# An S4 macaron block on one core: the opening by chunks, packing in lumps, and the S4 response as two products

## The chip, the core and the metric

The kernel runs on one NeuronCore of a Trainium2 chip. The core has a matrix engine (PE, TensorE), a vector engine (DVE), an activation engine (ACT), GpSimd (POOL) and SyncE (SP), which here issues most transfers. [...] The metric is the device time of one execution in microseconds (us), taken as the median of several; the profile shows one further execution.

## The reference

The input is 2048 tokens of 1024 features. Three blocks follow each other, each on a layer norm of `x`:

```python
x = x + 0.5 * ffn(layernorm(x))          # 4-bit weights, 1024 -> 2752 -> 1024
x = x + s4(layernorm(x))                 # long convolution along the features
x = x + 0.5 * ffn(layernorm(x))          # the same weights again

# ffn: W[k, n] = scale[k // 128, n] * (w4[k, n] - (z4[k // 128, n] + 1))
h = silu(xf @ Wg) * (xf @ Wu);  out = h @ Wd

# s4: the response K (1024 taps) from 64 poles, then a causal convolution plus D * u
at_roots = c * (k00 - k01 * (1 / (1 + k11)) * k10);  K = ifft(at_roots).real
y = irfft(rfft(u, 2048) * rfft(K, 2048), 2048)[..., :1024] + D * u
```

## The kernel before

The tokens are cut into four blocks of 512. Each of the two feed-forward layers on each block is a "job", eight in all (`JOBS`). A job has an up stage of 64 steps and a down stage of 44. The 2752 gate and up columns are cut into eight waves (`WAVES`): five of six units (a unit is 128 columns of gate or up), two of four and one of five. A wave has eight steps, one for each group of 128 rows that share a scale. In a step, each unit gets two matmuls of 128 x 512 into its own PSUM bank: one with the high part of the turned rows (`xTh`), one with the low part (`xTl`). Then the bank is multiplied in place by the ratio of two groups' scales (`scaled`, L618 to L622), on ACT for gate units and on DVE for up units, and only then can the next step's matmul add to it.

The weights arrive as 4-bit words. In job 0 they are unpacked once: for wave w, `fetch` (L441) loads the words and `fetch_zeros` (L448) the zero points, broadcast from a table in DRAM; `split` (L472, through `signed_bytes`, L455) makes bytes of them in six DVE operations; `dequantize` (L495) copies each of eight nibble positions into a contiguous tile `q` (a pool of four buffers) and stores it to DRAM as rows of `wq`. Every step of every job then loads 128 rows of bytes (`load_bytes`, L572) and casts them to fp32 (`make_weights`, L589): on POOL, in job 0 for steps 1, 2 and 5 of a wave on ACT, and the first one on DVE. A load of wave w waits for all eight stores of that wave. When a wave ends, `gated` (L675) makes the hidden rows and splits them into high and low halves, `hh` and `hl`, on POOL.

The order of work is made of three things. The function `at` hangs pieces of side work on steps of the up and down stages. A scheduler then orders the instructions of each engine by when it thinks them ready. `in_order_of_writing` (L140) ties the instructions of the named engines, so that they stay in the order in which they were written. `first_weights` (L537) hangs the packing of waves 1 to 7 on the steps of job 0: for wave w, with `s0 = 8 * w - 12`, it fetches at `s0 - 5`, splits in six pieces over `s0 - 3` to `s0 - 1`, and casts one nibble position a step from `s0` on.

Before all steps stands `start` (L1434): it loads the zero words, the rows of block 0 and the words of waves 0 and 1, makes the zero-point tables and sends them through DRAM, takes the moments of the four row tiles on DVE (`moments`, L175), packs wave 0, normalizes the first half of each row tile on ACT in two passes (`less_mean`, `by_deviation`), and turns it tile by tile on PE (`turn`, L230). The second halves follow in steps 0 to 3 (`second_half`, L1428). The pieces of wave 0 that step 0 needs go straight into a tile (`first_tile`), by transfers that POOL issues.

In job 1, `s4_tables` (L1014) makes the S4 tables in 63 pieces of side work. One part is `s4_response` (L940): it forms the 1024 taps of K from a table `se` of 128 x 2 x 8 numbers and two cosine and sine tables of 128 x 1024, one row of 128 taps at a time; two matmuls (cosine, sine) for each of eight rows, with one column of `se` as weights. The taps lie in a single partition and are stored to DRAM as one row, which `s4_toeplitz` reads back in 128 shifted copies.

## Time and profile before

| what | value |
|---|---|
| time, median of 3 (lowest to highest) | 2151.65 us (2150.85 to 2152.0) |
| the profiled execution: its own time, and its span | 2152.6 us, 2150.7 us |
| busy: PE, DVE, ACT, POOL | 2092.5, 1704.3, 1422.3, 1062.5 us |
| moved by DMA | 132.49 MB |
| chain of work that ended last | PE 87%, DVE 7%, POOL 2% |
| PE busy in 29 to 64, 64 to 88, 88 to 110.5, 110.5 to 133.3 us | 29.91, 22.66, 21.86, 22.45 us |
| DVE busy in the same stretches | 26.50, 22.41, 18.95, 19.70 us |

A table by stage gives, for each stretch of the span, the busy time of PE, of PE's weight loads, of DVE, ACT and POOL, the granted clock of PE, the share of the DMA engines and GB/s. The chain of work that ended last is followed back from the last instruction to whatever released each one; its lines are start, length and what. A timeline line is start, length, engine, source line, operation, tiles, shapes and count, with the idle time before it in brackets. A line of a group of instructions ends in busy time, mean duration in ns, and the engine's idle time before it with what ended most of that. SPq is an issue of a transfer by SP. Matmuls overlap, so the duration of one is longer than the distance to the next.

### The profile page before, as it was taken

What the parts mean: (1) busy time and instruction counts of PE and PEld (TensorE: products, weight loads), DVE (VectorE), ACT (ScalarE), POOL (GpSimd) and SP (SyncE); (2) the same over time, 40 slices, a digit from 0 to 9 for tenths busy, and PEclk for the clock granted to TensorE, in tenths of its full rate; (3) what the DMA queues carried; (4) which work ended last, traced back from release to release, by engine and by line L of the source; (5) the groups of instructions that cost most, each with busy time, mean ns of one, the idle gap of its engine ahead of it and who ended that gap; (6) DMA issues with size and microseconds to landing.
All of it is one profiled execution on the core that took longest, in us unless ns stands there. A gap on an engine that the chain in (4) does not pass through costs nothing.

```text
span 2150.7 us, 30258 instructions
## 1 busy us (share of the span) xinstructions
PE 2092.5 (97%) x9748; PEld 1425.5 (66%) x9748; DVE 1704.3 (79%) x2783; ACT 1422.3 (66%) x2233; POOL 1062.5 (49%) x1420
## 2 busy tenths in 40 slices
PE   4999999999999999999999999999999999999998
PEld 2555675577867568665776568676686766866576
DVE  7888978578788877778777788878788787777776
ACT  5887677646654776676767767646776467767765
POOL 3767747554344543455335553454534455345642
PEclk9999999999999999999999999999999999999999
DMA  4425232112111211212221121112111121121111
GB/s 136 116 85 148 78 92 59 32 54 76 41 41 54 89 53 39 78 33 58 87 80 36 31 74 37 38 52 77 35 36 41 52 93 48 44 81 36 34 35 57
DMA packets 163544, 132.49 MB, mean 62 GB/s; under 512 B 22252, under 2 KB 151029, under 8 KB 163376
## 3 DMA queue, kind: packets, MB, share of 16 engines
q1 hardware_dynamic: 162528, 129.12, 19.9%
q8 instruction: 79, 1.29, 0.3%
q10 hardware_dynamic: 592, 1.25, 0.2%
q14 instruction: 89, 0.73, 0.1%
q0 software_dynamic: 256, 0.10, 0.0%
HBM read 104.79 MB, written 25.50 MB: 61 GB/s over the span
## 4 chain that ended last, share of the span: by engine, by line
PE 87%; DVE 7%; POOL 2%; issue 1%; DMA 1%; ACT 1%; SPq 0%; DVEq 0%; ACTq 0%; POOLq 0%
PE pg L650 53%; PE po L713 27%; PE pc L1040 3%; DVE pg L622 2%; PE pb L735 1%; PE pb L1040 1%; PE pt L224 1%; DVE po L622 1%; PE st L224 1%; POOL w_down L598 0%; DVE hf L680 0%; POOL qd L531 0%; PE s_k L954 0%; DVE even L465 0%; ACT g L677 0%
## 5 line engine op out<-in xcount | busy, mean ns | idle before, releaser
L620 ACT ACTIVATE pg<-pg,rat 128x512 f32<-128x512 f32 x1240 | 787.3, 661 | 435.7 <-PE pg L650 434.8
L622 DVE TENSOR_TENSOR pg<-pg,rat 128x512 f32<-128x512 f32 x1168 | 776.1, 693 | 182.4 <-PE pg L650 178.4
L650 PE MATMUL pg<-xTh,w_up 128*128 128x512 f32 x2752 | 852.3, 438 | 6.3 <-DVE pg L622 4.5
L650 PE MATMUL pg<-xTl,w_up 128*128 128x512 f16 x2752 | 723.2, 383 | 13.6 <-DVE w_up L594 6.6
L650 PEld LDWEIGHTS pg<-xTh,w_up 128*128 128x128 f32 x2752 | 520.2, 189 | 185.2 <-DVE pg L622 18.3
L598 POOL CAST w_up<-b 128x768 fp32r<-128x768 int8 (+2 forms) x487 | 377.6, 781 | 529.6 <-PE pg L650 428.6
L713 PE MATMUL po<-hl,w_down 128*128 128x512 f32 x1344 | 538.8, 403 | 9.4 <-DVE po L622 7.3
L620 ACT ACTIVATE po<-po,ratd 128x512 f32<-128x512 f32 x660 | 431.0, 662 | 158.9 <-PE po L713 158.7
L713 PE MATMUL po<-hh,w_down 128*128 128x512 f32 x1344 | 522.4, 391 | 0.0
L622 DVE TENSOR_TENSOR po<-po,ratd 128x512 f32<-128x512 f32 x620 | 427.0, 697 | 96.6 <-PE po L713 92.6
L650 PEld LDWEIGHTS <-w_up 128*128 128x128 bf16 x2752 | 228.4, 99 | 335.3 <-issue 153.1
L598 POOL CAST w_down<-bd 128x512 fp32r<-128x512 int8 x352 | 222.5, 634 | 405.3 <-PE po L713 340.7
L713 PEld LDWEIGHTS po<-hl,w_down 128*128 128x128 f32 x1344 | 251.9, 188 | 86.2 <-DVE po L622 20.5
L713 PEld LDWEIGHTS po<-hh,w_down 128*128 128x128 f32 x1344 | 252.8, 188 | 45.2
L684 POOL TENSOR_TENSOR hl<-hf,hh 128x512 fp32r<-128x512 f32 x168 | 217.0, 1292 | 7.9
L680 DVE SCALAR_TENSOR_TENSOR hf<-pg,rat,g 128x512 f32<-128x512 f32 x168 | 122.9, 748 | 47.0 <-ACT g L677 37.4
L677 ACT ACTIVATE g<-pg,rat 128x512 f32<-128x512 f32 x168 | 110.6, 687 | 48.8 <-PE pg L650 38.9
L682 POOL CAST hh<-hf 128x512 fp32r<-128x512 f32 x168 | 106.4, 633 | 62.6 <-PE pg L650 30.5
L186 DVE BATCH_NORM_STATS2 stats<-x 128x6 f32<-128x512 f32 x96 | 63.6, 676 | 0.5
L1070 DVE TENSOR_TENSOR x<-x,pc 128x512 f32<-128x512 f32 x32 | 21.9, 685 | 36.9 <-PE pc L1040 36.9
L224 PE MATMUL pt<-ident,xn 128*128 128x128 f32 x256 | 43.2, 282 | 7.7 <-ACT xn L1426 7.7
L1040 PEld LDWEIGHTS pc<-near,st 128*128 128x128 f32 x256 | 43.6, 190 | 7.9
(177 smaller groups left out, 1043.3 us busy)
## 6 DMA issues: line engine op xcount, KB each, us to landing
b<-wq SPq DMA_DIRECT2D x319, 96.0 KB
bd<-wdq SPq DMA_DIRECT2D x336, 64.0 KB
x<-in_L_attn_u_dram SPq DMA_DIRECT2D x30, 512.0 KB
b<-wq SPq DMA_DIRECT2D x128, 64.0 KB
xs<-x SPq DMA_DIRECT2D x16, 512.0 KB
x<-xs SPq DMA_DIRECT2D x16, 512.0 KB
out_dram<-x SPq DMA_DIRECT2D x16, 512.0 KB
b<-wq SPq DMA_DIRECT2D x64, 80.0 KB
```

What stands on the lines that cost most here:

```text
L186: nc.vector.bn_stats(stats[:, t, i, :], x[b][t][:, bass.ts(i, 512)])
L224: nc.tensor.transpose(ps[:, bass.ts(k, P)], n[:, bass.ts(k, P)], ident)
L598: nc.gpsimd.tensor_copy(t, b)
L620: nc.scalar.activation(dst, src, AF.Copy, scale=sc)
L622: nc.vector.tensor_tensor(dst, src, sc.to_broadcast([P, TB]), ALU.mult)
L650: nc.tensor.matmul(p, weights, (lo, hi)[k][:, g, :], start=(g == 0 and not done), stop=(g == GK - 1 and done), skip_group_check=True,)
L677: nc.scalar.activation(g, pg, AF.Silu, scale=rat[:, 2 * f, GK - 1 :])
L680: nc.vector.scalar_tensor_tensor(hf, pu, last, g, ALU.mult, ALU.mult)
L682: nc.gpsimd.tensor_copy(hi, hf)
L684: nc.gpsimd.tensor_tensor(lo, hf, hi.bitcast(F32), ALU.subtract)
L713: nc.tensor.matmul(ps[c], w[:, bass.ts(c, P)], part, start=(f == 0 and k == 0), stop=(f == NF - 1), skip_group_check=True,)
L1040: nc.tensor.matmul(dst, lhsT, rhs, start=start, stop=stop, skip_group_check=True)
```

## The change

It has three parts.

The opening. `start` now loads wave 0's zero words straight from the input, broadcast to all partitions (`first_zero_words`), and the words of wave 0 ahead of the rows, gate on SP and up on ACT. `first_split` unpacks those zero words on DVE, so that wave 0 needs no table through DRAM, packs wave 0, and casts its odd nibble positions on POOL and its even ones on ACT, which subtracts 128 from unsigned bytes where DVE had one more xor; SP issues the transfers into `first_tile`. Moments of row tiles 1 and 3 are made on ACT (a sum, and a sum of squares of the centred rows), of 0 and 2 on DVE (`first_moments`). Rows are normalized in one pass, on ACT for odd and on DVE for even tiles, and turned chunk by chunk of 128 columns over all four tiles (`first_turn`): chunk 0 and 1 before step 0, chunks 2 to 7 at steps 0 to 5 (`rows_by_chunk`). `keep_warm` puts transposes of no use on PE, 18 ahead of chunk 0 and 6 behind it. The zero-point table of gate and up is made behind chunk 1, that of down at step 12. The first three weight casts are on POOL. PE joins the engines whose order in `start` is as written.

Packing in lumps. Waves 2 to 7 are fetched at `s0 - 3`, split in one piece at `s0 - 1`, and wave 2 begins at step 7 in place of 4, with two nibble positions a step.

The response. `se` is turned by the angle of each column (`m0` to `m3`, four products, a sum and a difference on POOL), so that one cosine and one sine table of 128 x 128 serve all eight columns: two matmuls with the table as weights and 8 moving columns give the taps as 128 x 8, which is stored as 128 pieces of 32 bytes.

```diff
         for w in range(1, len(WAVES)):
-            s0 = 8 * w - 12
+            s0 = 8 * w - 12 if w != 2 else 7
             if w > 1:
                 both = lambda w=w: (fetch(w), fetch_zeros(w))
-                at(up, max(0, s0 - 5), lambda both=both: in_order_of_writing(both, ET.SP))
-                steps = [(up, max(1, s0 - d)) for d in (3, 2, 2, 1, 1, 1)]
-                in_pieces(at, steps, lambda w=w: split(w))
+                at(up, s0 - 3, lambda both=both: in_order_of_writing(both, ET.SP))
+                in_pieces(at, [(up, s0 - 1)], lambda w=w: split(w))
...
-                s = s0 + j if w > 1 else j // 2
+                s = s0 + j if w > 2 else j // 2 + s0 * (w - 1)
                 at(up, s, lambda w=w, j=j: dequantize(w, j))
...
-        if i == 0:
-            nc.vector.tensor_copy(t, b)
-        elif j == 0 and stage == "up" and s % GK in (1, 2, 5):
+        if j == 0 and stage == "up" and s > 2 and s % GK in (1, 2, 5):
             nc.scalar.copy(t, b)
...
-                    nc.tensor.matmul(
-                        ps[:1, bass.ts(r, P)],
-                        s4["se"][:, i, 4 * half + r : 4 * half + r + 1],
-                        tables[i].rearrange("p (a r) -> p r a", r=8)[:, 4 * half + r, :],
...
+        nc.gpsimd.tensor_tensor(m0, se[:, 0, :], cos, ALU.mult)
+        nc.gpsimd.tensor_tensor(m1, se[:, 1, :], sin, ALU.mult)
+        nc.gpsimd.tensor_tensor(m2, se[:, 1, :], cos, ALU.mult)
+        nc.gpsimd.tensor_tensor(m3, se[:, 0, :], sin, ALU.mult)
+        yield
+        nc.gpsimd.tensor_tensor(m0, m0, m1, ALU.add)
+        nc.gpsimd.tensor_tensor(m2, m2, m3, ALU.subtract)
+        yield
+        ps = bank("s4_k")
+        for i, part in enumerate((m0, m2)):
+            table = tables[i].rearrange("p (a r) -> p r a", r=8)[:, 0, :]
+            nc.tensor.matmul(ps[:, :8], table, part, start=(i == 0), stop=(i == 1))
...
+        nc.sync.dma_start(k_dram[:, P - 1 :].rearrange("o (a r) -> (o a) r", r=8), k)
...
+    def first_moments():
...
+        for i, t in enumerate((1, 3)):
+            mean = mv[:, t, 0:1]
+            nc.scalar.activation(scratch, x[0][t], AF.Copy, scale=1.0 / HID, accum_out=mean)
+            nc.scalar.activation(
+                scratch, x[0][t], AF.Square, bias=mean, scale=-1.0, accum_out=squares[:, i : i + 1]
+            )
...
+    def first_rows(t, lo, hi):
...
+        if t % 2:
+            nc.scalar.activation(n, src, AF.Identity, bias=first["bias"][:, t : t + 1], scale=r)
+        else:
+            nc.vector.tensor_scalar(n, src, m, r, ALU.subtract, ALU.mult)
...
+    def first_turn(c):
...
+        for t in range(NT):
+            src = first[t, c // 4][:, bass.ts(c % 4, P)]
+            nc.tensor.transpose(ps[:, bass.ts(t, P)], src, ident)
+        nc.scalar.copy(hi, ps)
+        nc.vector.tensor_tensor(lo, ps, hi.bitcast(F32), ALU.subtract)
...
+        def dequantize(j):
+            q = qpool.tile([P, n], I8, tag="q", name=f"q_0_{j}")
...
+            if j % 2:
+                nc.gpsimd.tensor_copy(q, view(raw, I8))
+            else:
+                nc.scalar.activation(q, view(even, U8), AF.Identity, bias=minus_128)
+            nc.sync.dma_start(first_tile[j:P:8], q[: P // 8])
+            nc.sync.dma_start(w_q[0].rearrange("(r j) n -> j r n", j=8)[j], q)
...
     def start():
+        zq = first_zero_words()
+        first["x"] = x[0] = [t4(f"x_0_{t}") for t in range(NT)]
+        fetch(0, (nc.sync, nc.scalar))
+        for t, src in enumerate(rows_of(u, 0)):
+            (nc.sync, nc.scalar)[t % 2].dma_start(x[0][t], src)
...
+        dequantize_first = first_split(zq)
+        mv, scratch = first_moments()
+        for j in (1, 3, 5, 7, 0, 2, 4, 6):
+            dequantize_first(j)
         fetch(1)
         rows_next = scale_rows(3, 9)
+        keep_warm(18, scratch)
...
+        first_turn(0)
+        keep_warm(6)
+        for t in range(NT):
+            first_rows(t, P, 512)
+        scales(0, 3, srow)
+        first_turn(1)
         zero_points(0, zeros)
```

## The prediction

> **What bounds the kernel now.** I read the page's busy shares and slices first, for the engine that is never free.

> ```profile
> PE 2092.5 (97%) x9748; PEld 1425.5 (66%) x9748; DVE 1704.3 (79%) x2783; ACT 1422.3 (66%) x2233; POOL 1062.5 (49%) x1420
> PE   4999999999999999999999999999999999999998
> ```

> PE idles 58 us of 2150.7, and the first slice (54 us) holds over half. So a gain must either fill the opening or take work off PE. The table by stage comes next (PE, PEld, DVE, ACT, POOL busy, then clock, DMA share, GB/s).

> ```profile
> 0.00:20.00 20.00, 2.44 (x11) 1.96 (x11) 12.96 (x40) 6.28 (x9) 2.23 (x8) 1.00 0.56 198
> 20.00:40.00 20.00, 13.18 (x60) 8.17 (x60) 15.45 (x38) 15.31 (x27) 8.84 (x13) 1.00 0.29 83
> 40.00:60.00 20.00, 14.95 (x52) 7.52 (x51) 15.93 (x29) 10.33 (x17) 14.57 (x17) 0.83 0.47 140
> 60.00:80.00 20.00, 18.66 (x83) 10.78 (x82) 16.83 (x25) 15.82 (x25) 14.26 (x15) 1.00 0.37 102
> ```

> PE is idle 29.4 us in the first 60 and nearly full afterwards. The chain that ended last tells why (start, length, what):

> ```profile
> 1.33 4.88 DMA zq<-in_L_ffn_up_qzeros_dram
> ...
> 16.89 0.97 DVE even L465
> ...
> 22.39 2.06 DMA b<-q
> ...
> 25.67 2.39 DVE xTl L247 x4
> ...
> 29.04 3.11 PE pg L650 x7
> ...
> 43.17 4.83 DMA z<-z_dram
> ...
> 48.09 0.96 DVE even L465
> ...
> 49.71 19.41 PE pg L650 x71
> ```

> First matmul of the gate and up stage: 29.04. Before it stands one DVE queue: zero points, moments, packing, low parts. Then, at 43 to 49.7, DVE waits in its packing of wave 2 for that wave's zero points, with the scaling of PSUM banks queued behind it. PE stops, and the clock row reads 0.50 from 50.0 to 55.9. By counting matmuls (12 a step), step 8 starts at 63.98, step 16 at 87.82.

> **The change, part by part.** Durations are rows of before; the order on each engine is that of the two built programs.

> *Opening up to the first matmul.* The packed words and broadcast zero words are now fetched ahead of the rows. ACT's first transfer (issued 0.75) lets SP go on at 4.25, so DVE starts at 4.0. Unpacking 8 x 0.16 (43 columns took 0.84 for eight; 96 are wider), table 1.0 (688 halfwords took 0.52, now 1536), shifts 0.53 + 0.56, sums 2 x 0.95, one xor 0.56: 9.9. POOL then casts q1, q3, q5, q7 at 0.83 each: 13.2. ACT has x1 at about 7 and x3 at 8.5 (2.5 MB at some 0.38 MB/us from 1.8, the rate at which the first 10 us move data). Its four passes of 1024 columns have no row; two 512-column passes less one fixed part give 1.07 each, and adding an accumulator may add 0.2 (bounds 4.3 to 5.1 for the four, I take 4.4): 12. But its q0, q2, q4, q6 need the four q buffers, so each waits for a store of POOL's q to land, about 2.0 after issue (a 16-row piece took 2.06): they run at 13.2, 14.1, 15.0, 15.9 and end at 16.75. DVE has finished moments (2 x 1.45) and 15 tiny operations (2.9) at 15.7, so **ACT is late by a microsecond**: its rows come at 17.4, the first turn at 17.9, its eviction 18.5, low part 19.2, the 384-column rows by 20.0, and eight more transposes at 0.213: the first matmul at 21.3. The weight path (last q 16.75, piece landed 18.9, POOL cast 0.83) is ready at 19.8 and hidden. **-7.7.**

> *Warm-up transposes.* [...]

> ```profile
> 17.85 1.97 PE L224 MATMUL pt<-ident,xn 128*128 128x128 f32 x8 [7.21 <-ACT xn L1426]
> ...
> 31.98 0.60 PE L224 MATMUL pt<-ident,xn 128*128 128x128 f32 x4
> ...
> 42.52 1.22 SPq L452 DMA_DIRECT2D z<-z_dram  x2
> ...
> 43.84 8.98 SPq L503 DMA_DIRECT2D wq<-q  x7
> ```

> Eight transposes take 0.21 each from start to start; those at 31.98 take 0.11, after 2.9 us of matmuls. The clock row says 1.00 for both, so the spacing is the witness: 16 transposes over 4.2 us left PE at half speed, 7 matmuls woke it. [...] the new warming instructions are transposes. [...] Were they to warm it, 2.7; DVE, next in line, would let through 1.5 of the 2.5. I take 0.

> *Steps 0 to 7.* DVE sets the pace. From 22.6 it has, by these rows,

> ```profile
> L622 DVE TENSOR_TENSOR pg<-pg,rat 128x512 f32<-128x512 f32 x19 | 12.6, 690 | 5.4 <-PE pg L650 5.2
> L499 POOL COPY q<-raw 128x768 int8<-128x768 int8 x12 | 10.0, 831 | 1.0 <-DVE raw L467 1.0
> ```

> 19 bank scalings (13.1), six low parts (4.1), packing of waves 1 and 2 (8.6), scales (2.4), zero points (1.4), second rows (1.0): 30.6, plus waits of about 2.5: for PE's cold step 0 (1.4), for the zero points of wave 1 (ACT issues their table behind three bank scalings, 25.4; landed 27.3; read back about 4 later), and of wave 2. It ends at 55.7; PE's order puts nine matmuls of steps 8 and 9 ahead of the last of step 7, so step 8 starts in effect at 54.5, against 63.98: **-9.5** with the 7.7 in it. The old stall at 43 and the cold clock go; most of that is refilled by work that used to lie before 29.

> *Wave 3, the new wait.* Its fetch moves from step 7 to 9, on SP behind wave 2's store of q5. POOL gets to wave 2's casts only when DVE has split it (52.8), and then meets the three high and low halves of wave 0: q0 1.49 beside DVE, a wait for the odd bytes until 55.0, then 10.7 of work (five q, three hh 0.63, three hl 1.29, one cast). q5 at 65.8, words and zeros issued from 66.1. Before, such a pair issued at 41.55 had landed at 48.0; I take 6.1: 72.2. On DVE the split stands in front of step 12's bank scaling; 0.95 + 0.42 + 0.56 + 0.95 + 0.69 later pg_9 is free, at 75.9. PE, there at 66.8 plus 13 matmuls it can do, idles from 70.2: 5 to 6 us. Waves 1 to 3 in sum: step 16 starts near 83.3, 28.8 after step 8, where it was 23.8: **+5** (0 if POOL is early, +9 if the clock halves).

> *Lumps of waves 4 to 7.* Six packing operations (4.1 us; 2.9 at 512 columns) now lie between the scalings of one step, not three. A bank has 1.2 us of slack; by that the third scaling is 1.8 late, against 0.9. PE's order moves later matmuls forward. 0 to +5; I take **+2**. Fetch and split are still two steps apart, but from wave 3 on POOL's casts stand ahead of the halves, so these waits stay hidden.

> *Response (job 1).* A single-column weight with 128 moving columns, 32 passes, gives way to two products with 8 moving columns (four passes), like the sums at 374:

> ```profile
> 399.25:403.15 3.90, 3.87 (x16) 1.53 (x16) 1.00 0.06 17
> 405.85:409.75 3.90, 3.87 (x16) 1.53 (x16) 1.00 0.08 21
> ...
> 374.00:376.20 2.20, 1.95 (x16) 1.86 (x16) 1.00 0.15 44
> ```

> 7.74 becomes 4 x 0.122 = 0.49. PE is busy 105.0 of the 105 us from 400, so it is all time: **-7.2**. Six POOL operations of 0.2 stand before the halves; DVE loses two of 1.1; the row goes out as 128 pieces of 32 bytes, hidden by four loads in advance.

> *Moved at no cost:* zero points of down (step 12; behind wave 3's wait), first casts on POOL (idle there).

> Sum: -9.5 + 5 + 2 - 7.2 = -9.7. The profiled execution took 2152.6 around its span of 2150.7; I take the difference off the median 2151.65: **2142**. A measurement of this kernel can't tell 0.2% (4.3 us) from nothing.

> **Rivals.** *No wait in wave 3* (0.24): POOL reaches q5 three or more us earlier, or the zeros land faster (before, the opening's four pieces landed within 4). Then 2142 - 5, less what lumps don't cost: 2135. Against it: the chain of POOL work is made of measured rows. *Opening given back* (0.09): q buffers come free later, PE's idle in step 13 passes the length that halved the clock at 49, and lumps cost their 5: +6.5, 2148.5. *Response hidden* (0.06): another engine paces job 1; 2149. PE at 105 of 105 speaks against. *Slower* (0.06): the wait of wave 3 returns in each of waves 3 to 7, since each fetch stands behind a store of the wave before. Five waits of 5.6 are 28, 23 more than counted, 2165; from four waits on (+17 in place of the 5) the rest is eaten. Against it: only wave 2's casts meet halves in POOL's order.

> **How the numbers follow.** Mine has 0.55, own range 2138 to 2146. Adding the second rival's 2135 and the two at 2149 gives 2134 to 2150; beyond lie the slower case and half of the tails. Faster than 2147.3: 0.55 x 0.97 + 0.24 + a quarter of 0.15 + a little = 0.83; within 0.2%: 0.11; slower: 0.06.

> **What would show it.** First matmul near 21.3, held by ACT's rows; its first matmuls 0.43 apart; step 8 near 54.5; SP's fetch for wave 3 behind q5 near 66, DVE idle on the zeros, PE idle some 5 us near 70; no row of 32 passes near 400. I am wrong if PE is kept waiting in waves 4 to 7, or if the first matmul isn't before 24.

## The result, and the profile after

The changed kernel takes **2140.35 us** (median of 5 runs, 2137.67 to 2143.59) against 2151.65 (2150.85 to 2152.32): ratio 0.9947, 95% interval 0.9932 to 0.9961, that is 8 to 15 us less. Forecast were 2142 with a range of 2134 to 2150. The profiled execution took 2140.35 around a span of 2138.6.

First the page: busy time, and the slices of PE.

```profile
PE 2089.9 (98%) x9744; PEld 1426.0 (67%) x9744; DVE 1700.3 (80%) x2785; ACT 1420.2 (66%) x2233; POOL 1055.2 (49%) x1424
PE   6899999999999999999999999999999999999998
```

PE's busy time fell by 2.6 us only, although the response took 7.1 us off it: 24 warming transposes, 5.14 us of PE's busy time, were added. Its idle time fell from 58.2 to 48.7. The table by stage (PE, PEld, DVE, ACT, POOL busy, then clock, DMA share, GB/s):

```profile
0.00:20.00 20.00, 6.07 (x31) 5.84 (x31) 12.09 (x39) 11.91 (x19) 3.92 (x12) 1.00 0.48 169
20.00:40.00 20.00, 15.26 (x76) 9.29 (x77) 19.60 (x41) 13.46 (x23) 10.94 (x13) 0.98 0.35 106
40.00:60.00 20.00, 19.61 (x82) 10.32 (x81) 18.34 (x30) 14.78 (x24) 9.95 (x13) 0.93 0.43 124
60.00:80.00 20.00, 15.94 (x63) 8.54 (x63) 14.69 (x28) 11.06 (x18) 13.71 (x17) 0.84 0.35 105
```

The hole at 40 to 60 us (PE 14.95 of 20 before) is filled, though the clock is down to 0.93 there, and a new one has opened at 60 to 80 (15.94 of 20, 18.66 before). The chain of work that ended last (start, length, what) shows what holds each place:

```profile
8.81 2.37 POOL q L493 x3
...
19.85 1.35 DVE xn L1490 x2
...
28.36 3.76 DMA z<-z_dram
...
68.40 4.61 DMA z<-z_dram
...
73.03 0.96 DVE even L511
...
76.32 15.12 PE pg L689 x57
```

The packing comes first, then the rows and the first turn; the wait for wave 1's zero points at 28; and at 68 the wait for **wave 3's**, which the kernel before didn't have.

Since runs of one kernel differ by some 5 us, the experiments are read by stage: start of a step of job 0 (12 matmuls counted as a step, as in the prediction), and the length of job 1's gate and up stage from its first matmul to the next stage's. R1 is the changed kernel run once more.

```
                          step 0  step 8 step 12 step 16 step 24 step 40 step 56  job 1   median
before                     29.04   63.98   76.27   87.82  110.43  155.48  205.68  200.05  2151.65
changed                    21.75   53.19   65.06   83.52  106.45  150.36  199.91  192.93  2140.35
R1 changed again           21.70   53.24   64.74   83.70  105.47  149.39  200.90  191.47  2140.07
E1 response alone          30.57   65.40   77.67   89.24  111.78  156.81  205.61  193.57  2144.60
E2 wave 3's fetch early    21.15   53.10   64.62   82.23  104.24  148.07  196.87  191.35  2139.13
E3 pieces in waves 4 to 7  21.43   52.97   65.17   84.19  106.66  151.64  200.67  192.46  2141.40
E4 waves as before         21.41   57.22   68.64   83.19  106.05  151.05  200.33  193.13  2141.30
E5 two transposes          21.91   54.25   66.95   84.57  107.49  151.32  200.46  193.98  2140.92
E6 moments on DVE          21.19   55.81   67.85   87.23  110.13  153.97  202.64  191.47  2140.71
E7 E2, zeros of down late  21.15   51.55   63.63   80.74  102.93  146.76  195.85  191.52  2135.44
E8 E7, two casts on ACT    21.04   52.38   64.53   78.63  100.82  144.65  193.55  193.39  2134.55
R2 E8 again                21.21   53.19   64.28   79.24  101.45  145.31  194.49  191.29  2135.14
E9 two casts on ACT alone  21.19   53.08   64.89   82.59  104.53  148.38  199.65  193.04  2137.66
```

Part of what differs between these rows is PE's clock and not the edit. The granted clock of the changed kernel and of E3, which do the same work up to here:

```profile
38.00:42.00 4.00, 3.64 (x13) 2.37 (x13) 4.00 (x8) 1.78 (x3) 4.00 (x6) 0.66 0.36 122
38.00:42.00 4.00, 3.52 (x17) 2.17 (x17) 4.00 (x9) 2.40 (x4) 4.00 (x6) 1.00 0.36 123
```

In all eleven profiles of the new opening PE idles 2.2 us near 36 us (38 in E6). In six of them the clock falls behind that (changed, R1, R2, E2, E6, E9; it reads 0.66 in the first row above, 0.61 in E2), and steps 3 to 5 take 10.8 to 11.2 us; in the other five they take 9.75. Job 1 has such a place too, near 370 us: its steps 24 to 28 take 12.4 us in the six profiles with a halved clock there (before, changed, E4, E5, E8, E9; it reads 0.59 from 376 to 380 in the kernel before, 0.78 from 372 to 376 in the changed one) and 10.8 in the other seven.

### The profile page after: what moved, and what is told of

Same layout as the page of the kernel before. It is cut to its first block, busy times and chain, and to the rows that moved or that the text cites. A ratio compares the mean times of both kernels' runs of the same rounds, so it can differ in the third digit from the quotient of the medians.

```text
span 2138.6 us, 30244 instructions
## 1 busy us (share of the span) xinstructions
PE 2089.9 (98%) x9744; PEld 1426.0 (67%) x9744; DVE 1700.3 (80%) x2785; ACT 1420.2 (66%) x2233; POOL 1055.2 (49%) x1424
## 3 DMA queue, kind: packets, MB, share of 16 engines
q1 hardware_dynamic: 162646, 128.65, 19.8%
q8 instruction: 79, 1.29, 0.3%
## 4 chain that ended last, share of the span: by engine, by line
PE 89%; DVE 6%; POOL 2%; DMA 1%; issue 1%; ACT 1%; SPq 0%; ACTq 0%; DVEq 0%; POOLq 0%
PE pg L689 54%; PE po L752 27%; PE pc L1078 3%; PE pb L774 1%; DVE pg L661 1%; PE pb L1078 1%; PE pt L228 1%; DVE po L661 1%; PE st L228 1%; DMA wq<-q 0%; DMA z<-z_dram 0%; DVE hf L719 0%; DVE hf_half L733 0%; DVE rawd L511 0%; POOL w_down L637 0%
## 5 line engine op out<-in xcount | busy, mean ns | idle before, releaser
L689 PEld LDWEIGHTS pg<-xTh,w_up 128*128 128x128 f32 x2752 | 520.3, 189 | 180.3 <-DVE pg L661 17.6
L752 PEld LDWEIGHTS po<-hl,w_down 128*128 128x128 f32 x1344 | 252.0, 188 | 85.9 <-DVE po L661 19.8
L187 DVE BATCH_NORM_STATS2 stats<-x 128x6 f32<-128x512 f32 x88 | 58.5, 676 | 0.5
L776 DVE TENSOR_TENSOR x<-x,pb 128x512 f32<-128x512 f32 x64 | 43.1, 678 | 6.2 <-PE pb L774 6.2
```

What stands on the lines that cost most here:

```text
L187: nc.vector.bn_stats(stats[:, t, i, :], x[b][t][:, bass.ts(i, 512)])
L689: nc.tensor.matmul(p, weights, (lo, hi)[k][:, g, :], start=(g == 0 and not done), stop=(g == GK - 1 and done), skip_group_check=True,)
L752: nc.tensor.matmul(ps[c], w[:, bass.ts(c, P)], part, start=(f == 0 and k == 0), stop=(f == NF - 1), skip_group_check=True,)
L776: nc.vector.tensor_tensor(part, part, ps, ALU.add)
```

## The experiments

**E1, the response alone** (the kernel before with the new `s4_response`, nothing else).

```diff
-        for half in range(2):
...
-                    nc.tensor.matmul(
-                        ps[:1, bass.ts(r, P)],
-                        s4["se"][:, i, 4 * half + r : 4 * half + r + 1],
...
+        for i, part in enumerate((m0, m2)):
+            table = tables[i].rearrange("p (a r) -> p r a", r=8)[:, 0, :]
+            nc.tensor.matmul(ps[:, :8], table, part, start=(i == 0), stop=(i == 1))
...
```

> The kernel before with only the new response. Theory (the prediction's term): PE is the bound in job 1, and 7.74 us of single-column passes become about 0.5 us, so job 1's gate and up stage falls from 200.4 to 193.2 us and the whole by 7.2 us, to about 2144.5. Rival (response hidden): another engine paces job 1, the stage falls by less than 2 us and the time stays within 2 us of 2151.65.

Measured: 2144.6 us, ratio 0.9977 (0.9966 to 0.9988), so -4.9 us with an interval of -7.3 to -2.6. Job 1's stage itself shrinks from 200.05 to 193.57; in all twelve profiles with the new response it is 191.3 to 194.0. The steps that held the response show it without that scatter: steps 28 to 36 of job 1 take 29.4 us in the kernel before and 22.3 to 22.4 in all twelve, **7.1 less**. What stands in place of the 32 passes, in the changed kernel (duration least/median/most in ns, first and last start):

```profile
L1004 PE MATMUL s_k<-s_rest,s_tc x2: 192/287/382, 395.7 to 395.7; 128*128 128x8 f32 x2
L1004 PE MATMUL s_k<-s_rest,s_ts x2: 382/383/384, 396.0 to 396.2; 128*128 128x8 f32 x2
```

All four passes start within half a microsecond. PE was the bound and nothing took its place in these steps. Elsewhere in E1's stage two things nearly cancel: the clock near 370 us stayed whole (1.6 us less than in the kernel before), and steps 36 to 44 took 2.2 us more, where PE waits, among others, 0.83 us for the taps to be read back (`s_rows`, at 412 us). E5 has the same wait, 0.81 us; most profiles don't. The whole-run ratio alone would leave anything from 3 to 7 open.

**E2, wave 3's fetch early.**

```diff
-                at(up, s0 - 3, lambda both=both: in_order_of_writing(both, ET.SP))
+                at(up, s0 - (6 if w == 3 else 3), lambda both=both: in_order_of_writing(both, ET.SP))
```

> The changed kernel with wave 3's fetch issued at step 6 instead of 9, ahead of all of wave 2's stores. Theory: DVE's wait for wave 3's zero points (to 73.0), PE's 4 us of idle time at 70.75 and the half clock after it are all due to the fetch's place behind the store of q5; they go, step 16 starts near 77 instead of 83.5, and the whole is 6 to 7 us faster than the changed kernel, about 2134, with less spread from run to run. Rival (work refills the gap): DVE's work, not the wait, sets step 16; it moves by less than 2 us and the time stays near 2140.

First what it takes away. In the changed kernel SP issues wave 3's words only behind the store of q5, and DVE waits for words and zero points (start, length, queue or engine, line, what; in brackets the idle time before it and what ended it):

```profile
65.57 0.32 SPq L545 DMA_DIRECT2D wq<-q  x1
65.94 1.23 SPq L454 DMA_DIRECT2D raw<-_L_ffn_gate_qweight_dram  x1
...
67.75 1.23 SPq L461 DMA_DIRECT2D z<-z_dram  x2
```

DVE in the same stretch of the timeline:

```profile
69.97 0.56 DVE L505 TENSOR_SCALAR even<-raw 128x768 int32<-128x768 int32 x1 [1.12 <-DMA raw<-in_L_ffn_up_qweight_dram]
...
73.03 0.96 DVE L511 TENSOR_TENSOR even<-even,z 128x1536 uint16<-128x1536 uint16 x1 [1.87 <-DMA z<-z_dram]
```

PE is idle from 70.75 to 74.04 and from 75.55 to 76.32, 4.1 us, and comes back at half clock, as the stage rows say:

```profile
70.00:74.00 4.00, 0.75 (x3) 0.28 (x2) 2.13 (x6) 1.82 (x4) 0.00 (x0) 0.93 0.44 136
74.00:78.00 4.00, 3.19 (x11) 1.76 (x12) 4.00 (x8) 0.00 (x0) 3.09 (x3) 0.50 0.36 98
```

With the fetch at 47 to 50 us neither wait is left, and the clock row reads 1.00 from 62 to 82 us. Yet PE still idles 1.6, 1.2 and 1.4 us between 66 and 77, now behind scalings on DVE and ACT; step 16 moves by 1.3 us only, from 83.5 to 82.2, and the whole (2139.1) can't be told from the changed kernel's. I had expected 6 to 7. The chain in E2 says where it went:

```profile
68.42 2.15 POOL q L544 x2
...
70.59 1.63 DMA wq<-q
...
72.44 0.32 SPq L621
...
72.81 2.24 DMA b<-wq
```

Step 16 is the first of wave 2's weights, and its load needs all eight q of wave 2. POOL casts the last of them at 69 to 70.6, because the three high and low halves of wave 0 lie between the casts; wave 2's first loads have landed by 75, and ACT, with the cast of its second weights at the head of the queue, stands 4.2 us with PSUM scalings behind it. DVE is no freer: its packing of wave 3, which no longer waits, now meets POOL's casts, and a sum that took 0.96 takes 2.03. **The wait on the zero points was one of three limits that end within 3 us of each other.**

**E7 and E8: E2, with the other two taken away one after the other.** E7 moves the zero points of down from step 12 to 22 (3.1 us of DVE); E8 has ACT cast q4 and q6 of wave 2.

```diff
-                at(up, 12, lambda: in_order_of_writing(zeros, ET.DVE, ET.SP))
+                at(up, 22, lambda: in_order_of_writing(zeros, ET.DVE, ET.SP))
```
```diff
-        nc.gpsimd.tensor_copy(q, packed[w][j % 2][:, j // 2, :])
+        copy = nc.scalar.copy if w == 2 and j in (4, 6) else nc.gpsimd.tensor_copy
+        copy(q, packed[w][j % 2][:, j // 2, :])
```

> The changed kernel with wave 3's fetch at step 6 and, besides, the zero points of down moved from step 12 to step 22. If DVE's work alone sets step 16 once the fetch is early (it was busy without a break from 62 to 76), the 3.1 us of unpacking taken out of it move step 16 from 82.2 to about 79.5. If the last cast of wave 2 on POOL sets it (its store landed at 72.2 and the load for step 16 stood behind it), step 16 stays near 82.

> As the one before it, and q4 and q6 of wave 2 are cast on ACT instead of POOL. If POOL's chain of wave 2 (casts between the high and low halves) is what holds the load for step 16, its last store lands 2 to 3 us earlier and step 16 starts near 77; the whole is 5 to 6 us faster than the changed kernel, near 2135. If the time then goes into the queue of ACT, whose bank scalings stand behind the casts, step 16 stays near 80.

E7: step 16 at 80.7. Of the 1.5 us, 1.0 was there at step 12 already, ahead of the moved work: E2 ran part of steps 3 to 5 at half clock (11.2 us), E7 didn't (9.75). So DVE's zero points account for 0.5 (steps 12 to 16 take 17.1 us, 17.6 in E2): DVE's work alone was not the limit. E8: steps 12 to 16 take 14.1 us, 3.0 less, step 16 at 78.6, the whole 2134.55, ratio 0.9929 (0.9915 to 0.9944). POOL's chain was the larger of the limits that remained. It doesn't reach the 77 that I expected: steps 12 to 16 would take 10.8 us at 2.7 a step, as in steps 24 to 40.

**E9, the two casts on ACT alone** (the second edit of E8 on the changed kernel, with the fetch and the zero points where they were).

> The changed kernel with q4 and q6 of wave 2 cast on ACT, nothing else. If POOL's chain in wave 2 is the root of the loss near 70 us, the store of q5 and with it wave 3's fetch go out 2 us or more earlier than 65.6, DVE's waits (1.1 and 1.9 us) shrink to under 1, and step 16 starts near 80.5; the total is 2 to 3 us faster than the changed kernel, near 2137.5. If the fetch's place in the queue is a loss of its own, DVE and PE still wait some 3 us near 70 and step 16 stays at 83.

SP's fetch goes out at 63.9 instead of 65.9, as expected, but DVE still waits, 3.2 us for the words alone (69.16; 4.4 us after their issue had ended, where the changed kernel took 2.3 — why, no run here settles), PE idles 1.8 and 1.8 us, and the clock reads 0.50 from 74 to 78. Step 16 at 82.6, 1 us earlier; the whole 2137.7, ratio 0.9936 (0.9923 to 0.9950). So neither cure does alone what the three edits do together: early fetch 1.3 us at step 16, casts on ACT 1.0, all three 4.9 (E8) and 4.5 (R2, against R1 beside it; both with the halved clock near 40 us, which E8 lacks). Early fetch and casts without the moved zero points were not run together.

**R1 and R2, the changed kernel and E8 again, on one chip.**

> The changed kernel once more, beside the two variants of this call. The steps from 24 to 56 should repeat within 0.5 us (93.5), as in all kernels with lumps; PE's idle time near 70 us and the half clock behind it should come back, with step 16 at 82.5 to 84.5; the total near 2140.

> The kernel with the early fetch, the late zero points and q4 and q6 on ACT once more, beside the changed kernel on the same chip: step 16 near 78.6, steps 24 to 56 at 92.7, the total 4 to 6 us faster than the changed kernel. If the gain of the earlier comparison was the chip's, less than 2 us.

2140.07 (2136.83 to 2141.09) and 2135.14 (2131.18 to 2136.31): the two sets of runs don't overlap, and against the kernel before the variant's ratio is 0.9926 (0.9912 to 0.9940), the changed kernel's 0.9946 (0.9932 to 0.9960). The wait and the half clock near 70 us came back in R1 (0.50 from 76 to 80), step 16 at 83.70. What I had wrong: steps 24 to 56 of R1 took 95.4 us, not 93.5; up to step 48 they repeat to 0.01 us (67.52), but steps 48 to 56 took 27.9 where they took 25.9 before. The clock tells the two apart (changed kernel, then R1):

```profile
178.00:182.00 4.00, 2.74 (x11) 1.30 (x12) 3.74 (x8) 1.93 (x4) 2.60 (x5) 1.00 0.66 185
178.00:182.00 4.00, 3.28 (x11) 1.47 (x11) 2.90 (x5) 2.50 (x4) 3.01 (x5) 0.71 0.47 127
```

E9, at 27.7 us, has it too (0.57 in the same row); in the seven other profiles with lumps the clock stays at 1.00 there, and they take 25.1 to 25.9. What comes before it is the same in all nine: a pause of PE of 1.1 to 1.5 us, and up to 0.7 more, of which E3 tells.

**E4, the waves as before** (wave 2 packed in steps 1 to 3 and cast in steps 4 to 11, pieces, fetches at s0 - 5), opening and response new.

```diff
-            s0 = 8 * w - 12 if w != 2 else 7
+            s0 = 8 * w - 12
...
-                at(up, s0 - 3, lambda both=both: in_order_of_writing(both, ET.SP))
-                in_pieces(at, [(up, s0 - 1)], lambda w=w: split(w))
+                at(up, max(0, s0 - 5), lambda both=both: in_order_of_writing(both, ET.SP))
+                steps = [(up, max(1, s0 - d)) for d in (3, 2, 2, 1, 1, 1)]
+                in_pieces(at, steps, lambda w=w: split(w))
...
-                s = s0 + j if w > 2 else j // 2 + s0 * (w - 1)
+                s = s0 + j if w > 1 else j // 2
```

> The changed kernel with the order of the waves as before (wave 2 packed in steps 1 to 3 and cast in steps 4 to 11, fetches at s0 - 5, pieces); opening and response stay new. Theory: without the late fetch there is no wait in wave 3 and the opening's gain is kept: step 16 near 78.5, the whole 5 us faster than the changed kernel, about 2135. Rival: DVE meets the zero points of wave 2 too early, as at 43 us in the kernel before, and PE idles 5 us there and loses its clock: step 16 near 84, the time near 2140.

The rival came true: DVE meets wave 2's zero points 1.06 us too early at 43.3, PE idles 3.1 us in four pieces between 44.2 and 49.7, the clock falls to 0.57 at 50 to 54, step 8 comes at 57.2. There is no late fetch in wave 3 here, and steps 12 to 16 take 14.6 us in place of 18.5; step 16 lands at 83.2, within 0.3 us of the changed kernel. The change's own order of waves moves the stall from wave 2 to wave 3; it doesn't remove it.

**E3, pieces in waves 4 to 7.**

```diff
-                at(up, s0 - 3, lambda both=both: in_order_of_writing(both, ET.SP))
-                in_pieces(at, [(up, s0 - 1)], lambda w=w: split(w))
+                at(up, s0 - (5 if w > 3 else 3), lambda both=both: in_order_of_writing(both, ET.SP))
+                steps = [(up, s0 - d) for d in ((3, 2, 2, 1, 1, 1) if w > 3 else (1,))]
+                in_pieces(at, steps, lambda w=w: split(w))
```

> The changed kernel with the packing of waves 4 to 7 in six pieces over three steps and their fetch at s0 - 5, as before; waves 2 and 3 stay. By the prediction's term (lumps cost 2 us) it is 2 us faster, steps 16 to 56 taking 114 us instead of 116.4. By the changed kernel's trace, where these steps took 1.5 us less than before, the lumps cost nothing and it is 0 to 1.5 us slower. Steps 0 to 15 are as in the changed kernel.

Steps 24 to 40 settle it: 45.05, 45.03, 44.98 and 45.00 us in the four kernels with pieces (before, E1, E3, E4), 43.83 to 43.92 in the nine with lumps. **Lumps are 1.15 us faster over these two waves**, 0.58 each. In steps 40 to 48, where wave 7 is packed, they are faster by another 2.0: 25.63 to 25.66 with pieces, 23.58 to 23.61 with lumps. Steps 48 to 56 take it back: 23.2 to 24.6 with pieces, 25.1 to 25.9 with lumps, 27.7 and 27.9 in the two with the halved clock. Over steps 24 to 56 that leaves 93.8 to 95.3 with pieces and 92.5 to 93.5 with lumps, 95.1 and 95.4 in those two. The timeline of DVE in E3, at the packing of wave 5:

```profile
110.33 1.15 DVE L505 TENSOR_SCALAR even<-raw 128x512 int32<-128x512 int32 x1
...
113.52 1.31 DVE L511 TENSOR_TENSOR even<-even,z 128x1024 uint16<-128x1024 uint16 x1
114.75 1.88 DVE L662 TENSOR_TENSOR pg<-pg,rat 128x512 f32<-128x512 f32 x3
```

The same two operations in the changed kernel's lump:

```profile
115.51 0.42 DVE L505 TENSOR_SCALAR even<-raw 128x512 int32<-128x512 int32 x1
...
116.78 0.68 DVE L511 TENSOR_TENSOR even<-even,z 128x1024 uint16<-128x1024 uint16 x1
```

The pieces lie up to two steps earlier. There POOL is making the high and low halves of the wave that just ended and a weight cast (109.2 to 114.3), and the two operations take 1.15 and 1.31 us beside it, where the lump, in a stretch in which POOL is idle (115.65 to 117.46), takes 0.42 and 0.68. PE then waits 0.37 us at 115.1 for the scaling behind the sum; in the changed kernel its chain runs through from 105.95 to 122.82. The lump isn't even solid: DVE's order puts a scaling after every one or two of its operations.

What takes the gain back stands behind step 48. The first two lines are DVE's packing of the down weights, the same sum in the changed kernel and in E3; the others are PE in the changed kernel:

```profile
176.26 1.76 DVE L511 TENSOR_TENSOR rawd<-rawd,zd 128x1024 uint16<-128x1024 uint16 x1
179.12 0.68 DVE L511 TENSOR_TENSOR rawd<-rawd,zd 128x1024 uint16<-128x1024 uint16 x1
...
178.69 0.51 PE L689 MATMUL pg<-xTh,w_up 128*128 128x512 f32 x1 [1.50 <-DVE pg L661]
...
180.66 0.82 PE L689 MATMUL pg<-xTl,w_up 128*128 128x512 f16 x3 [0.57 <-POOL w_up L637]
```

In the changed kernel the sum lies beside POOL's work on a low half of wave 5 (176.14 to 177.48), and the scaling behind it is late; then PE waits for the first weights of wave 7, whose load stands behind the store of the last q (cast at 174.04, landed at 179.8). In E3 that q is cast at 171.67 and PE has neither wait. No experiment moved these two apart, so that they are the whole loss is read from the traces and not shown.

**E5, one warming transpose in place of 18, and one in place of 6.**

```diff
-        keep_warm(18, scratch)
+        keep_warm(1, scratch)
...
-        keep_warm(6)
+        keep_warm(1)
```

> The changed kernel with one warming transpose in place of 18 and one in place of 6. If transposes wake PE, as the trace of the changed kernel has it (spacing 0.213 us until 18.72, 0.109 from 18.88, with no matmul in between), the transposes at 20 us are 0.213 apart and the first three us of matmuls 0.43 apart, so that step 1 starts some 2 us later; DVE, next in line, takes part of it and step 8 is 0 to 1.5 us later. If transposes don't count, [...] the spacings stay and nothing moves. The total stays within 2 us of the changed kernel either way.

The timeline of PE in the changed kernel:

```profile
17.44 1.06 PE L1503 MATMUL pt<-ident,xn 128*128 128x128 f32 x4
18.30 1.07 PE L1517 MATMUL warm<-ident 128*128 128x128 f32 x6
...
20.29 0.66 PE L1503 MATMUL pt<-ident,xn 128*128 128x128 f32 x4 [0.64 <-DVE xn L1490]
...
21.75 0.81 PE L689 MATMUL pg<-xTl,w_up 128*128 128x512 f16 x3
```

The same in E5:

```profile
20.15 1.97 PE L1503 MATMUL pt<-ident,xn 128*128 128x128 f32 x8 [1.15 <-DVE xn L1490]
21.91 1.49 PE L689 MATMUL pg<-xTl,w_up 128*128 128x512 f16 x3
```

In the changed kernel the transposes start 0.213 us apart from 13.8 to 18.7 and 0.109 apart from 18.9 on, with no matmul in between, and the first matmuls follow at 0.216. In E5 the transposes at 20 are 0.213 apart, and the first matmuls 0.43 until 23.6. So transposes alone brought the full clock here, 25 of them in a row, 5.2 us after the first. The prediction had taken them not to count, on 16 in the kernel before that stayed 0.21 apart; the measurement says the contrary. What it is worth is small: step 1 comes 1.1 us later without it, but step 3 doesn't (33.90 against 34.18, and 34.26 in R1), so it is all gone in PE's waits for DVE, which is next in line. Steps 8 and 16 do come 1.0 us later, behind something else: DVE waits 2.23 us for wave 2's zero points (to 52.6; 0.55 us in the changed kernel, to 51.3), and PE idles 2.06 us. Whether their later fetch goes back to the cold start, no run shows. The total (2140.9 against 2140.35 and 2140.07) can't tell.

**E6, moments of all four tiles on DVE.** ACT's four passes are left out, DVE computes the statistics of tiles 1 and 3 too, and the warming transposes read a row tile.

```diff
-        for i, t in enumerate((1, 3)):
-            mean = mv[:, t, 0:1]
-            nc.scalar.activation(scratch, x[0][t], AF.Copy, scale=1.0 / HID, accum_out=mean)
...
-        for t in (0, 2):
+        for t in range(NT):
...
-        nc.vector.tensor_scalar(mv[:, 1:4:2, 1], squares, 1.0 / HID, None, ALU.mult)
...
-        keep_warm(18, scratch)
+        keep_warm(18, first["x"][3])
```

> The changed kernel with the moments of all four tiles on DVE. DVE gets 3.0 us more work ahead of the first matmul, of which 1.35 fills the idle time in which it waits for ACT's sums (12.1 to 13.5); ACT's casts of q move forward to about 10.5. The deviations are ready at 17.6 instead of 16.3, the first matmul comes 1.0 to 1.5 us later, near 23, and since DVE paces steps 0 to 7, step 8 is as much later. If q's path by ACT and the loads of the first weights set the first matmul instead, it is unchanged or earlier.

The first matmul is not later (21.19): here the weights' path sets it, and the chain runs through SP's stores. SP issues a pair (first tile's rows, and the store) every 1.22 us, from 9.7 to 18.9; the last piece lands at 20.1, and POOL's cast ends at 21.1. In the changed kernel this path was ready at 20.99, only 0.8 us before the first matmul. Later it falls behind: step 8 at 55.8 (+2.6), step 16 at 87.2 (+3.7). But the edit did two things. DVE has more work; and the warming transposes, fed by a row tile, now run from 10.7 to 14.2 us. Their spacing goes from 0.213 to 0.109 after 2.9 us, so they brought the full clock here too; then PE idles 3.3 us, and the clock is down to 0.50 when the first matmuls come:

```profile
20.00:24.00 4.00, 3.23 (x15) 2.60 (x15) 3.31 (x11) 1.12 (x2) 1.40 (x2) 0.50 0.72 217
```

Step 1 comes at 28.04, 3.2 us after the changed kernel's. So the 2.6 and 3.7 us are the moments and the half clock together, and this run doesn't part them. The total, 2140.7, shows neither: by the table E6 has made up 1.0 us of the 3.7 by step 56 and another 1.5 in job 1, where its clock stayed whole.

## Why the prediction was right, point by point

*Opening, -7.7 at the first matmul and -9.5 at step 8.* Measured -7.3 (21.75) and -10.8 in the changed kernel (-10.7 in R1); no run traces the 1.3 more at step 8 to a term, and the old opening scatters too: E1, which has it unchanged, starts at 30.57 and reaches step 8 at 65.40. The new opening was not run alone; E4, with the waves as before, starts at 21.41. Inside the first number three terms were off and balanced: DVE's packing ended at 8.75, not 9.9; ACT got its first row tile at 8.56, not 7, and its four passes with their reads of the accumulator (1.06 us a sum, 1.15 a sum of squares, 0.18 to 0.19 a read) took 4.88 us, not 4.4, so that its casts began at 13.34 as the passes ended (forecast were passes to 12.0 and a wait for q buffers to 13.2); the weights' path was ready at 21.0, not 19.8, because SP took 1.22 us for each pair of stores. ACT's rows held the first turn, as forecast (16.89 to 17.75); DVE's 384-column rows (to 21.2) were the last ahead of the matmuls.

*Warming transposes, 0.* Wrong in mechanism (E5). I put step 0 at 0.43 us a matmul, 5.2 us in all (2.7 if warm), and my witness in the kernel before, 16 transposes that stayed 0.21 us apart, came in three groups with idle time between them and stopped 4.4 us after they began. The sum survives because DVE, next in line, lets nothing of it through by step 3, where the prediction would have let through 1.5 of the 2.5 us that it put between a cold step 0 and a warm one.

*Wave 3's wait, +5.* The mechanism is there to the microsecond: q5's store at 65.6 (65.8 forecast), fetch from 65.9 (66.1), zero points at 73.0 (72.2), PE idle from 70.75 (70.2), step 16 at 83.5 (83.3). Two things failed in it. PE idled 4.1 us, not 5 to 6, but the clock fell to 0.50, which I had kept for the upper end only: steps 8 to 16 took 30.3 us, so the term was +6.5, and step 16 came within 0.2 us of the forecast because the opening had gained 1.3 more than forecast. That agreement is luck. And the step was told as one wait with one remedy, where E2, E8 and E9 show three limits together: the fetch's place, POOL's chain of wave 2, and DVE beside POOL. The rival without the wait was priced at 5 us less for it, and 2135 in all; with the wait taken out the time was 2139.1. It took the other two edits to come to 2135.

*Lumps, +2.* Of the wrong sign: -1.15 over steps 24 to 40 and -2.0 over steps 40 to 48, of which steps 48 to 56 took back 1.4 (changed kernel against kernel before). I counted packing operations between scalings and gave each its lone duration; what costs, by the rows of E3, is which POOL work they meet: a sum of 1024 halfwords took 0.68 us with POOL idle, 1.31 beside a weight cast and 1.76 beside a low half. What makes it so, no run here shows.

*Response, -7.2.* Measured -7.1 in steps 28 to 36 of job 1, in every profile; the whole stage, with its clock, gave -7.1 in the changed kernel and -6.5 in E1.

*Sum, -9.7.* Measured -12.1 in span and -11.3 in median. Of the profile's difference, -4.3 lie before step 16 (-4.5 forecast), -1.5 in steps 16 to 56 (+2 forecast), -7.1 in job 1, and +0.8 in all the rest. So the response and the first matmul were right in mechanism and size; the opening's and wave 3's misses cancelled; the lumps' sign was wrong by more than the 2.4 us that the sum missed. The rival that the wait returns in waves 3 to 7 came true in small: PE is not idle 0.3 us at a stretch between 97.1 and 177.2, but at the passage to wave 7 it waits 1.50 and 0.57 us. By the prediction's own sign ("if PE is kept waiting in waves 4 to 7") that counts against it; what saves the sum is that the kernel before waits no less: PE's pauses of 0.3 us and more from step 24 on, to the end of job 0's up stage, come to 3.5 us there and to 2.9 in the changed kernel.

## What to carry to other kernels

Where a wait is forecast at a place at which several engines are nearly full, look for what comes next before pricing its removal: here the wait was 3 us of DVE's time and 4 of PE's, its removal gave 1.3, and only the third edit in a row gave 4.9. Price an operation that is moved by what the other engines do at that moment (the same shift on DVE took 0.42 us in the lump, 1.15 beside POOL's halves), not by its mean. And when runs of a kernel scatter by 5 us, compare by counted steps: steps 24 to 40 repeat to 0.1 us over nine profiles, and told a term of 1.15 us that no total could. Where a stage itself scatters by 1 or 2 us, look at the granted clock before calling it noise: job 1's steps 24 to 28 took 12.4 us with the clock down and 10.8 without.

## What the runs showed of the hardware

The same pause didn't always cost the clock. Behind PE's 2.2 us near 36 us it fell in six of eleven profiles (0.66 from 38 to 42 in the changed kernel, 1.00 in E3), and behind 1.1 to 1.5 us near 178, with up to 0.7 more, in two of nine (0.71 from 178 to 182 in R1, 1.00 in the changed kernel). E2's 1.6, 1.2 and 1.4 us between 66 and 77 left it at 1.00; E9's 1.8 us at 69.6 were followed by 0.68 from 72 to 74 and 0.50 from 74 to 78. Summed from the clock rows, with a halved clock at 0.50, the changed kernel ran at half clock for 3.4 us in 38 to 46 (4 us rows of 0.66 and 0.91) and for 6.8 in 70 to 82 (0.93, 0.50, 0.72), the kernel before for 6.8 in 48 to 56 (2 us rows of 0.76, 0.50, 0.50, 0.54).

DVE and POOL were slower side by side: a sum of 1536 halfwords on DVE took 0.96 us with POOL idle (changed kernel, 73.03) and 2.03 beside POOL's casts and a low half (E2, 65.25), and in that stretch of E2 a cast on POOL took 1.55 us, 0.83 in the changed kernel.
